# One level more of the fast product inside two of seven products, in ten slots of a gated FFN's last batch

## The chip, the cores and the metric

One core of one Trainium2 chip. The metric is the device time of one execution in microseconds (us). The kernel before took 711.19 us, the median of three runs (712.08, 711.18, 711.19). The profile is of one execution on the same core.

## The reference

A feed-forward layer with a gate, a conditioned norm ahead of it and 8-bit quantised hidden values behind it, cut to what matters:

```python
# x: (4, 1024, 512)   cond: (4, 128)   norm_w: (512, 128)
# up_w: (4096, 512)   down_w: (512, 2048)
scale = cond @ norm_w.T + 1.0
ms = jnp.mean(x * x, axis=-1, keepdims=True)
h = x * (scale[:, None, :] * jax.lax.rsqrt(ms + 1e-6))
u = h @ up_w.T
val, gate = jnp.split(u, 2, axis=-1)
h = val * jax.nn.gelu(gate, approximate=False)
# per token: 127 / max|h|, rounded and clipped, divided again
hq = act_quant(h)
# one scale for all: rounded to -1, 0, 1
wq = weight_quant(down_w)
return hq @ wq.T + x
```

## The kernel before, in words

The four batches (b = 0 to 3) of 1024 tokens go one after the other. A batch has 16 slots. A slot makes 128 of the 2048 hidden columns, gate and value, for all 1024 tokens: 2 x 2 blocks (gate or value, first or second 512 tokens) over an inner length of 512. Each slot uses one level of Winograd's form of Strassen's product: seven products of half the size in every direction instead of eight. A product is six matmuls of 128x128 weights with 512 tokens (`product`, L698 to L706; TERMS: each operand is split into a high and a low float16 part, of which three combinations count, times two halves of the inner length of 256). So a slot is 42 matmuls.

The steps of a slot are the methods of class `Slot` (L801 to L862). In the names below A, B and E are banks of PSUM, and v, t1 and t2 are float32 tiles of 128x512:

- `first` makes product 0 in A, and the scalar engine copies it to B (`first_copy`, L812). `fourth` makes product 4 in E, copied to v (L820). `fifth` adds product 5 onto A, copied to t2 (L827).
- `second` adds product 1 onto B: this is a gate half, whose Gelu goes to t1 (`second_gelu`, L834). `third` adds product 3 onto A. VectorE multiplies this value half by t1 and writes the hidden values H (`third_out`, L840).
- `gate` adds product 2 onto E, VectorE adds t2 (`gate_sum`, L848), and the scalar engine takes its Gelu (`gate_gelu`, L851). `value` adds product 6 onto A, VectorE adds v (`value_sum`, L857) and multiplies the two (`value_out`, L860).

`slot` (L864) writes these steps down in an order in which the first half of a slot stands between the second half of the one before. Each engine runs its instructions in the order of the code. Between the steps are places called x, y and z, into which other work is put. PSUM has two banks A, one B, two E and three that are called po, for the down projection.

While one batch runs, the batch before it is quantised and projected down. `pair_max` (L901) takes the largest absolute value over a pair of slots (L911), and merges it into a running maximum (L913). After the last pair GpSimd takes the maximum over the partitions (`token_max`, L927). VectorE makes the scales from it, and then multiplies each piece, two slots times 512 tokens, by them (`quant_scale`, L993). Either VectorE rounds the piece (`quant_round`, L997) or the scalar engine does in two steps (`quant_up`, L1001, `quant_down`, L1005). The down projection has small matmuls (L1070) over sums of such pieces (class `Pair`, L1049 to L1058). In the last batch only the sums are made beside the slots, for batch 2's projection, which runs in the tail behind the last slot. A class `Filler` (L1470) holds the maxima and pieces in a list with costs, and gives them out at x, y and z as its budget for a slot allows. GpSimd has nothing to do in the last batch's slots.

The parts of the weights wait in DRAM. `s_load_x` and `s_load_y` (L495 to L502) bring them in for each slot, some by a transposing DMA (L489), on the queue of SyncE (SP).

## Time and profile before

| | |
|---|---|
| runs | 712.08, 711.18, 711.19 us; median 711.19 |
| profiled execution | span 710.3 us from the first to the last instruction; the page gives no other time of it |
| median less span | 0.9 us |
| granted TensorE clock | 1.000 |
| busy: TensorE, VectorE, scalar engine, GpSimd | 703.8, 593.1, 421.9, 155.0 us |
| last batch's slots 0 and 4 begin at | 507.23, 543.50 us |
| a slot | 9.07 us |

The page's first part gives the busy time, the share of the span and the number of instructions of each engine (PE is TensorE, PEld its weight loads, DVE VectorE, ACT the scalar engine, POOL GpSimd). A group's row gives line, engine, operation, output and input tiles, shape, count, then busy us, mean ns of one, and the idle time ahead with what ended it. A timeline's row gives start, length, engine and line, and in brackets the idle time ahead of it and what released it. "issue" means that nothing which the profile shows was waited for.

### The profile page before, as it was taken

To read this page: it belongs to the slowest core of one execution; us is meant where nothing else is said; L and a number is where in the kernel's file an instruction comes from. 1 tells how busy PE (TensorE), PEld (TensorE's weight loads), DVE (VectorE), ACT (ScalarE), POOL (GpSimd) and SP (SyncE) were. 2 spreads that over 40 slices of the span, in tenths; PEclk is the share of its full clock that TensorE was granted. 3 is DMA by queue.
4 is the path that set the end of the run, shared out by engine and by line. 5 is a ranking of instruction groups with operands and counts; after the bars stand their busy time and mean duration, and the time that the engine had idled before them with its cause. 6 is when DMAs were issued, how large, how long until landed. Compare 5 with 4: busy or idle time off the path is not lost.

```text
span 710.3 us, 10162 instructions
## 1 busy us (share of the span) xinstructions
PE 703.8 (99%) x3620; PEld 355.3 (50%) x3620; DVE 593.1 (84%) x881; ACT 421.9 (59%) x714; POOL 155.0 (22%) x162
## 2 busy tenths in 40 slices
PE   8999999999999999999999999999999999999998
PEld 4544444444444446664444446665444444445854
DVE  7999878899888799998798868977688888755896
ACT  6987798975777754534336675544334665332473
POOL 1444535551200405430200033440020000000120
PEclk9999999999999999999999999999999999999999
DMA  7989999899776766479344555786744444442253
GB/s 261 324 270 252 254 188 263 217 207 227 264 135 163 179 178 172 136 174 225 118 118 105 133 126 150 191 188 141 207 105 105 104 105 97 99 101 90 105 178 119
DMA packets 223188, 120.26 MB, mean 169 GB/s; under 512 B 185353, under 2 KB 194589, under 8 KB 223138
## 3 DMA queue, kind: packets, MB, share of 16 engines
q1 hardware_dynamic: 222986, 119.49, 65.7%
q8 instruction: 28, 0.46, 0.3%
q14 instruction: 22, 0.18, 0.1%
q10 hardware_dynamic: 152, 0.13, 0.1%
HBM read 52.32 MB, written 23.09 MB: 106 GB/s over the span
## 4 chain that ended last, share of the span: by engine, by line
PE 97%; DVE 1%; ACT 1%; DMA 1%; issue 0%; ACTq 0%; SPq 0%
PE A L703 43%; PE E L703 21%; PE B L703 11%; PE po L1070 9%; PE po_end L1022 4%; PE pg L718 3%; PE pv L718 3%; PE pz L1194 1%; DMA s_dram<-s_rows 1%; PE ptx L1178 1%; PE pv L791 0%; PE po_B L1070 0%; PE pg L791 0%; PE pw L388 0%; PE po_E L1070 0%
## 5 line engine op out<-in xcount | busy, mean ns | idle before, releaser
L703 PEld LDWEIGHTS <-SXY 128*128 128x128 f16 x2268 | 221.9, 98 | 260.3
L703 PE MATMUL A<-R,SXY 128*128 128x512 f16 x1170 | 270.7, 379 | 0.0
L703 PE MATMUL E<-R,SXY 128*128 128x512 f16 x606 | 147.1, 379 | 0.0
L840 DVE SCALAR_TENSOR_TENSOR H<-A,sg,t 128x512 f32<-128x512 f32 x59 | 44.2, 749 | 61.2 <-PE A L703 56.9
L703 PE MATMUL B<-R,SXY 128*128 128x512 f16 x324 | 78.8, 379 | 0.0
L993 DVE TENSOR_TENSOR H<-H,am 128x1024 f32<-128x1024 f32 x64 | 76.5, 1217 | 0.0
L851 ACT ACTIVATE t<-t,sg 128x512 f32<-128x512 f32 x59 | 42.5, 719 | 57.0 <-DVE t L848 56.9
L911 DVE TENSOR_REDUCE gm<-H 128x512 f32<-128x1024 f32 x56 | 69.3, 1237 | 1.0
L927 POOL PARTITION_ALL_REDUCE am<-R x8 | 14.3, 1793 | 228.8 <-DVE R L913 228.8
L834 ACT ACTIVATE t<-B,sg 128x512 f32<-128x512 f32 x59 | 40.5, 686 | 36.9 <-PE B L703 36.9
L827 ACT COPY t<-A 128x512 f32<-128x512 f32 x59 | 34.3, 581 | 43.3 <-PE A L703 42.5
L820 ACT COPY v<-E 128x512 f32<-128x512 f32 x59 | 34.6, 586 | 33.5 <-PE E L703 30.0
L860 DVE SCALAR_TENSOR_TENSOR H<-v,sg,t 128x512 f32<-128x512 f32 x59 | 47.1, 800 | 7.3 <-ACT t L851 6.9
L812 ACT COPY B<-A 128x512 f32<-128x512 f32 x59 | 33.8, 573 | 32.4 <-PE A L703 32.0
L857 DVE TENSOR_TENSOR v<-A,v 128x512 f32<-128x512 f32 x59 | 40.4, 685 | 14.9 <-PE A L703 13.0
L1070 PE MATMUL po<-wd,R 128*128 128x256 fp8e4 x416 | 52.4, 273 | 0.0
L1070 PEld LDWEIGHTS <-R 128*128 128x128 bf16 (+1 forms) x448 | 43.8, 98 | 8.9
L848 DVE TENSOR_TENSOR t<-E,t 128x512 f32<-128x512 f32 x59 | 39.9, 678 | 6.6 <-PE E L703 6.6
L913 DVE TENSOR_TENSOR R<-R,gm 128x512 f32<-128x512 f32 x56 | 41.7, 745 | 1.1
L578 POOL TENSOR_SCALAR ssq<-ssq 128x2 f32<-128x2 f32 x12 | 5.4, 451 | 164.1 <-ACT xt L608 116.1
L1001 ACT ACTIVATE H<-H 128x1024 f32<-128x1024 f32 x33 | 34.7, 1051 | 5.2 <-DVE H L993 5.2
L1005 ACT ACTIVATE R<-H 128x1024 bf16<-128x1024 f32 x33 | 34.8, 1056 | 0.7
(249 smaller groups left out, 928.2 us busy)
## 6 DMA issues: line engine op xcount, KB each, us to landing
SXY<-s_dram SPq DMA_DIRECT2D x45, 256.0 KB, 3.0
SXY<-s_dram SPq DMA_DIRECT2D x51, 128.0 KB, 3.1
xr<-in_x_dram SPq DMA_DIRECT2D x19, 256.0 KB, 3.0
out_dram<-xr SPq DMA_DIRECT2D x19, 256.0 KB, 2.6
H<-in_L_cond_up_w_dram SPq DMA_DIRECT2D x9, 512.0 KB, 4.3
H<-in_x_dram SPq DMA_DIRECT2D x8, 512.0 KB, 6.2
s_dram<-s_rows SPq DMA_DIRECT2D x16, 256.0 KB, 2.7
s_dram<-SXY SPq DMA_DIRECT2D x4, 896.0 KB, 4.5
```

What stands on the lines that cost most here:

```text
L703: PE.matmul(o, s[:, w, k, :], operand(g // NJ, c, l, k), start=start and n == 0, stop=stop and n == len(TERMS) - 1, skip_group_check=True,)
L718: PE.matmul(ps, a[k // 2][:, w, k % 2, :], XP[:, l, k, h * TOK : (h + 1) * TOK], start=n == 0, stop=n == len(terms) - 1,)
L834: ACT.activation(self.t1, self.B, AF.Gelu, scale=gain(self.g, 1))
L840: DVE.scalar_tensor_tensor(h_half(self.g, 0), self.A, gain(self.g, 0), self.t1, ALU.mult, ALU.mult)
L848: DVE.tensor_tensor(self.t2, self.E, self.t2, ALU.add)
L851: ACT.activation(self.t2, self.t2, AF.Gelu, scale=gain(self.g, 1))
L857: DVE.tensor_tensor(self.v, self.A, self.v, ALU.add)
L860: DVE.scalar_tensor_tensor(h_half(self.g, 1), self.v, gain(self.g, 0), self.t2, ALU.mult, ALU.mult)
L911: DVE.tensor_reduce(gm[0], v, AX.X, ALU.max, apply_absolute_value=True)
L913: return [largest, lambda: DVE.tensor_tensor(m, m, gm[0], ALU.max)]
L993: DVE.tensor_tensor(v, v, r.to_broadcast([P, 2, TOK]), ALU.mult)
L1070: PE.matmul(po, w[:, j], m, start=start and j == 0, stop=stop and j == n - 1, skip_group_check=True,)
```

## The change

In slots 4 to 13 of the last batch, products 0 and 4 (of the seven) are no longer made by slot. Two neighbouring slots, an even and an odd one, are taken as a pair: their weights for such a product, side by side, are a matrix of 256 columns, the inner length is 256, and there are 512 tokens. That is again cut in two in each direction, and made by seven inner products (class `Inner`) of three matmuls each, 128x128 weights by 256 tokens. These 21 replace twice six of 512 tokens. Five pairs are made this way (`two_slots`).

The inner products need sums of the weights and the tokens, split into high and low parts once more. The tokens' sums are made once, for product 0 on VectorE (in batch 2's slot 15; the low part in slot 0) and for product 4 on GpSimd (sums behind slot 0, the low part behind slot 2); the scalar engine makes the high parts (`two_tokens`). The weights' sums are made for each pair, on GpSimd, one pair ahead (`two_weights`), from rows that `two_load` brings; in exchange `s_load_x` leaves out products 0 and 4 there. The inner sums take more copies on the scalar engine, and four additions of 128x256 a pair on VectorE (`lower_left`, `lower_right`).

In the last batch the pieces, maxima and sums no longer come from the `Filler` but from a list (`TWO_PLAN`), each with a slot and a place. Seven scalings of pieces go to GpSimd (`"scale"`). In a pair `gate` of the slot before comes ahead of its `third`, and `third` is cut in two. The banks A of the even slot, Z0 and Z4 are those of the down projection. Batch 2's maxima of slots 12 and 13 may start in slot 14's z, and not only in slot 15's x. Slot 14 takes its first two banks from the down projection's. The factor on the tokens X_UP is halved and the factor that undoes it doubled.

The diff, cut to its core:

```diff
--- before.py
+++ after.py
-X_UP = 2.0**8
+X_UP = 2.0**7
...
+    TWO = range(4, 14)
+    TWO_1 = TWO.start // 2
+
+    def in_two(g):
+        return g // NJ == B - 1 and g % NJ in TWO
 
     def s_load_x(g):
+        if in_two(g):
+            s_load(g, Y_TO + 1, C_ALL)
+            s_load(g, 1, Y_FROM, True)
+            return
...
-    def product(c, g, ps, start, stop):
+    def product(c, g, ps, start, stop, n0=0, n1=6):
...
-        for n, (w, l, k) in enumerate(TERMS):
+        for n, (w, l, k) in list(enumerate(TERMS))[n0:n1]:
...
         def first(self):
-            self.A = bank("A", 2, name=f"A_{self.g}")
+            if self.g == LAST * NJ + TWO.stop:
+                self.A, self.E = (po_bank(f"{n}_{self.g}") for n in "AE")
+            else:
+                self.A = bank("A", 2, name=f"A_{self.g}")
...
+    def two_load(c, m):
+        r, n = two_raw(c, m), PLACE[c]
+        for i in range(2):
+            j = block(LAST * NJ + 2 * m + i)
+            d = s_dram[j, :, n * 2 * HALF : (n + 1) * 2 * HALF]
+            if c == 0 or j in TURNED:
+                SP.dma_start(out=r[:, i].rearrange("p w f -> p (w f)"), in_=d)
+            else:
+                SP.dma_start_transpose(r[:, i].rearrange("p w (k f) -> p (w k) f", k=2), d)
+
+    def two_tokens(c, eng):
+
+        f, o = two["f"], two["T", c]
+        t = t_view(LAST)[:, :, c]
+        v = [t[:, :, n].rearrange("p a k t -> p k a t") for n in range(2)]
+        b11, b12, b21, b22 = (f[:, n] for n in range(4))
+
+        def whole():
+            w = f.rearrange("p (k h) t -> p k (h t)", k=2).rearrange("p k (a t) -> p k a t", t=P)
+            eng.tensor_tensor(w, v[0], v[1], ALU.add)
+
+        def sums():
+            eng.tensor_tensor(b22, b22, b12, ALU.subtract)
+            eng.tensor_tensor(b12, b12, b11, ALU.subtract)
+            eng.tensor_tensor(b11, b22, b11, ALU.add)
+            eng.tensor_tensor(b21, b21, b11, ALU.subtract)
+
+        def high():
+            ACT.copy(o[:, :, 0], f)
+
+        def low():
+            eng.tensor_tensor(o[:, :, 1], f, o[:, :, 0], ALU.subtract)
+
+        return whole, sums, high, low
+
+    def two_weights(c, m):
+
+        r, o = two_raw(c, m), two["W", c]
+        g = two["v"] if m == TWO_1 else two["g"]
+        g = g.rearrange("p (n f) -> p n f", n=4)
+        a11, a12, a21, a22 = (g[:, n] for n in range(4))
+        w = g.rearrange("p (j k) f -> p j (k f)", j=2)
+
+        def sums():
+            POOL.tensor_tensor(w, r[:, :, 0], r[:, :, 1], ALU.add)
+            POOL.tensor_tensor(a11, a11, a21, ALU.subtract)
+            POOL.tensor_tensor(a21, a21, a22, ALU.add)
+            POOL.tensor_tensor(a22, a22, a11, ALU.subtract)
+            POOL.tensor_tensor(a12, a12, a22, ALU.subtract)
+
+        def split():
+            ACT.copy(o[:, :, 0], g)
+            POOL.tensor_tensor(o[:, :, 1], g, o[:, :, 0], ALU.subtract)
+
+        return sums, split
...
+        def product(self, a, b, bank, half, start=False):
+            o = bank[:, half * HALF : (half + 1) * HALF].rearrange("p (a t) -> p a t", t=P)
+            for n, (w, l) in enumerate(((1, 0), (0, 1), (0, 0))):
+                PE.matmul(
+                    o, self.weight(a, w), self.tokens(b, l), start=start and n == 0, stop=n == 2,
+                    skip_group_check=True,
+                )
+
+        def first(self):
+            self.product("A11", "B11", self.Z, 1, True)
+            self.product("S3", "T3", self.Z, 0, True)
+
+        def first_copy(self):
+            m1 = self.Z[:, HALF:].rearrange("p (y o) -> p y o", y=1).to_broadcast([P, 2, HALF])
+            ACT.copy(self.out.rearrange("p (y o) -> p y o", y=2), m1)
+            ACT.copy(self.v, self.Z[:, :HALF])
+
+        def second(self):
+            self.product("A22", "T4", self.Z, 0)
+            self.product("S2", "T2", self.out, 1)
+            self.product("A12", "B21", self.out, 0)
+
+        def second_copy(self):
+            ACT.copy(self.u, self.out[:, HALF:])
+
+        def third(self):
+            self.product("S1", "T1", self.out, 1)
+
+        def lower_left(self, o):
+            DVE.tensor_tensor(o[:, :HALF], self.Z[:, :HALF], self.u, ALU.add)
+
+        def lower_right(self, o):
+            DVE.tensor_tensor(o[:, HALF:], self.out[:, HALF:], self.v, ALU.add)
+
+        def fourth(self):
+            self.product("S4", "B22", self.out, 1)
...
+        e.A = po_bank(f"A_{g}")
+        z4 = po_bank(f"Z4_{g}")
+        z0 = po_bank(f"Z0_{g}")
+        e.E = bank("E", 2, name=f"E_{g}")
+        o.A = bank("A", 2, name=f"A_{g + 1}")
+        o.v = wpool.tile([P, TOK], F32, name=f"v_{g + 1}", tag="v")
+        uv = wpool.tile([P, 2, HALF], F32, name=f"uv_{g}", tag="t1")
+        p0 = Inner(0, m, z0, e.A, uv)
+        p4 = Inner(4, m, z4, e.E, two["uv", 4])
+        p0.first()
+        p4.first()
+        p0.first_copy()
+        p4.first_copy()
+        prev.gate()
+        prev.gate_sum()
+        run("x")
+        p0.second()
+        p4.second()
+        w0[0]()
+        p0.second_copy()
+        p4.second_copy()
+        if more:
+            two_load(4, m + 1)
+        p0.third()
+        p0.lower_left(o.A)
+        p0.lower_right(o.A)
+        prev.third(0, 3)
+        p4.third()
+        p4.lower_left(o.v)
+        p4.lower_right(o.v)
+        prev.gate_gelu()
+        p0.fourth()
+        prev.third(3, 6)
+        e.first_copy()
+        w0[1]()
+        p4.fourth()
+        w4[0]()
+        prev.value_out()
+        prev.third_out()
+        run("y")
+        e.fifth()
+        e.fifth_copy()
+        e.v = two["v"]
+        ACT.copy(e.v, e.E)
+        e.second()
+        e.second_gelu()
+        run("z")
+        e.value()
+        e.value_sum()
+        o.first_copy()
+        if m + 2 < TWO.stop // 2:
+            two_load(0, m + 2)
+        even("loads")
+        e.gate()
+        e.gate_sum()
+        ran("x")
+        o.fifth()
+        o.fifth_copy()
+        o.E = bank("E", 2, name=f"E_{g + 1}")
+        ACT.copy(o.E, o.v)
+        e.gate_gelu()
+        e.value_out()
+        w4[1]()
+        o.second()
+        o.second_gelu()
+        ran("y")
+        e.third()
+        e.third_out()
+        o.value()
+        o.value_sum()
+        ran("z")
+        odd("loads")
...
+    TWO_PLAN = [
...
+        (6, "y", "piece", (4, 0), (5, 0)), (7, "x", "max", (2, 0)), (7, "z", "max", (2, 1)),
+        (5, "x", "scale", (2, 1)), (5, "z", "scale", (3, 1)),
...
+            after_pair = (14, "z") if (b, i) == (LAST - 1, 6) else (2 * i + 3, "x")
...
+        if b == LAST:
+            steps[0, "x"] = [(two_tokens(0, DVE)[3], (1.25, 0))]
+            steps[2, "x"] = [(two_tokens(4, POOL)[2], (0, 1.06))]
...
+                    two_tokens(0, POOL)[2]()
...
+            if b + 2 == B and j == NJ - 1:
+                two_places()
+                for c in (0, 4):
+                    two_load(c, TWO_1)
+                fs = two_tokens(0, DVE)
+                steps[NJ - 1, "x"] = [(fs[0], (1.25, 0)), (fs[1], (1.8, 0))]
...
+            if b + 1 == B and j == 0:
+                for f in two_tokens(4, POOL)[:2]:
+                    f()
+            if b + 1 == B and j == 1:
+                two_weights(0, TWO_1)[0]()
+            if b + 1 == B and j == 2:
+                two_tokens(4, POOL)[3]()
```

Rows of the kernel after carry the changed kernel's line numbers. The scalar engine around the last batch's slot 2 (slots are counted through the batches here, so this is 50; `two_t4` is the tile of the token sums for product 4, `two_n` the float32 sums ahead of the split). Before:

```order
L812 COPY B_50_4977<-A_50_4970 128x512
L820 COPY v_50_4986<-E_50_4979 128x512
L834 ACTIVATE t1_50_4994<-B_50_4977,sg_3_4828 128x512
L827 COPY t2_50_5011<-A_50_4970 128x512
L851 ACTIVATE t2_49_4943<-t2_49_4943,sg_3_4828 128x512
L812 COPY B_51_5044<-A_51_5037 128x512
L820 COPY v_51_5053<-E_51_5046 128x512
```

After:

```order
L826 COPY B_50_5004<-A_50_4997 128x512
L835 COPY v_50_5013<-E_50_5006 128x512
L849 ACTIVATE t1_50_5021<-B_50_5004,sg_3_4843 128x512
L934 CAST two_t4_4766<-two_n_4768 128x4x256
L842 COPY t2_50_5041<-A_50_4997 128x512
L866 ACTIVATE t2_49_4965<-t2_49_4965,sg_3_4843 128x512
L826 COPY B_51_5073<-A_51_5066 128x512
L957 CAST two_w0_4767<-two_n_4768 128x4x128
```

A cast of the token sums, which GpSimd makes, now stands ahead of the copy of A to t2 of slot 2, and the first of the weights' casts ahead of slot 3's copy of E.

GpSimd from the last rows of batch 3's tokens on (`am_2` is the maximum over the partitions, `ready` a dummy of the same operation, `two_r0` raw weight rows, `two_w0` the weights made from them; a row "ISA" without operands is an instruction that stands ahead of each change of kind). Before:

```order
L637 TENSOR_TENSOR H_79<-H_79 128x256 x4
L920 ISA
L920 ISA ready_108<-ready_108 128x1
L927 ISA am_2_4830<-R_78 128x512 x2
L920 ISA ready_108<-ready_108 128x1
L927 ISA am_3_5919<-R_78 128x512
L962 ISA am_3_5919<-row_0_6019 128x512
```

After:

```order
L1165 ISA am_2_4845<-R_78 128x512 x2
L925 ISA
L925 TENSOR_TENSOR two_n_4768<-R_78 128x1024
L928 TENSOR_TENSOR two_n_4768<-two_n_4768 128x256
L929 TENSOR_TENSOR two_n_4768<-two_n_4768 128x256
L930 TENSOR_TENSOR two_n_4768<-two_n_4768 128x256
L931 TENSOR_TENSOR two_n_4768<-two_n_4768 128x256
L950 TENSOR_TENSOR two_n_4768<-two_r0_4769 128x512
L951 TENSOR_TENSOR two_n_4768<-two_n_4768 128x128
L952 TENSOR_TENSOR two_n_4768<-two_n_4768 128x128
L953 TENSOR_TENSOR two_n_4768<-two_n_4768 128x128
L954 TENSOR_TENSOR two_n_4768<-two_n_4768 128x128
```

Where the queue went on to the dummy for the tail, there are now the sums of the tokens and the weights, behind an operand-less row of their own. The low part of the tokens (`two_t4`) follows the last of these rows.

VectorE in slots 6 and 7 (54 and 55 and on). Before:

```order
L848 TENSOR_TENSOR t2_53_5218<-E_53_5183,t2_53_5218 128x512
L857 TENSOR_TENSOR v_54_5261<-A_54_5245,v_54_5261 128x512
L860 SCALAR_TENSOR_TENSOR H_79<-v_53_5190,sg_3_4828,t2_53_5218 128x512
L993 TENSOR_TENSOR H_79<-H_79,am_2_4830 128x2x512
L997 TENSOR_SCALAR R_78<-H_79 128x4x256
L840 SCALAR_TENSOR_TENSOR H_79<-A_54_5245,sg_3_4828,t1_54_5269 128x512
L906 TENSOR_REDUCE R_78<-H_79 128x512 x2
L911 TENSOR_REDUCE gm_3_1_0_5349<-H_79 128x512
L848 TENSOR_TENSOR t2_54_5289<-E_54_5254,t2_54_5289 128x512
L857 TENSOR_TENSOR v_55_5330<-A_55_5314,v_55_5330 128x512
L860 SCALAR_TENSOR_TENSOR H_79<-v_54_5261,sg_3_4828,t2_54_5289 128x512
```

After, behind slot 7's maxima, up to the even slot of the next pair (`Z0`, `Z4`: banks of inner products, `uv`: copies of inner products):

```order
L863 TENSOR_TENSOR t2_55_5475<-E_55_5477,t2_55_5475 128x512
L1011 TENSOR_TENSOR A_57_5520<-Z0_56_5518,uv_56_5522 128x256
L1014 TENSOR_TENSOR A_57_5520<-A_56_5516,uv_56_5522 128x256
L1011 TENSOR_TENSOR v_57_5521<-Z4_56_5517,two_n_4768 128x256
L1014 TENSOR_TENSOR v_57_5521<-E_56_5519,two_n_4768 128x256
L875 SCALAR_TENSOR_TENSOR H_79<-v_55_5334,sg_3_4843,t2_55_5475 128x512
L855 SCALAR_TENSOR_TENSOR H_79<-A_55_5333,sg_3_4843,t1_55_5489 128x512
L1231 TENSOR_TENSOR H_79<-H_79,am_2_4845 128x2x512
L1235 TENSOR_SCALAR R_78<-H_79 128x4x256
L1231 TENSOR_TENSOR H_79<-H_79,am_2_4845 128x2x512
L1235 TENSOR_SCALAR R_78<-H_79 128x4x256
L872 TENSOR_TENSOR two_n_4768<-A_56_5516,two_n_4768 128x512
```

The pieces stood one at a time between the outputs of slots. Now two stand together, scaled and rounded, behind the outputs of the odd slot, and four additions of 128x256 stand ahead of those.

146 lines of the change are left out of this document (125 added, 21 removed), and 13 rows, old and new, of the table TWO_PLAN.

## The prediction

> **What bounds the kernel now.** I read the page first, then the chain that ended last, then busy time by stretch in the last batch, then the groups by form, and last the timelines of the places that the change touches. The page:
>
> ```profile
> span 710.3 us, 10162 instructions
> PE 703.8 (99%) x3620; PEld 355.3 (50%) x3620; DVE 593.1 (84%) x881; ACT 421.9 (59%) x714; POOL 155.0 (22%) x162
> PE 97%; DVE 1%; ACT 1%; DMA 1%; issue 0%; ACTq 0%; SPq 0%
> ```
>
> TensorE is busy 99% of the span and 97% of the chain. So every stall that the change makes on PE is added in full, and every matmul that it saves is saved in full. The chain's pieces give the price of a matmul of each width (start, length, engine, line, count):
>
> ```profile
> 533.29 2.59 PE A L703 x12
> 652.43 1.75 PE po L1070 x16
> ```
>
> A 128x512 product matmul takes 2.59 / 12 = 0.216 us. The 256-column matmuls of the down projection take 1.75 / 16 = 0.109. Two slots of the last batch, one of those that the change rewrites first and one of the last (bounds, length, then busy time of PE, PEld, DVE, ACT, POOL):
>
> ```profile
> 545.12:554.19 9.07, 9.07 (x44) 4.12 (x42) 8.34 (x9) 5.81 (x9) 0.00 (x0) 1.00 0.44 104
> 617.68:626.75 9.07, 9.07 (x43) 4.09 (x42) 6.58 (x10) 3.16 (x6) 0.00 (x0) 1.00 0.45 101
> ```
>
> PE has no gap in either. VectorE stands at 8.34 of 9.07 in the first: it is the next engine to be late. GpSimd is idle throughout, at a granted clock of 1.00.
>
> **What it removes.** A pair of slots had 84 matmuls of 512 columns. It gets 60, and 42 of 256. That is 84 x 0.216 = 18.13 us before and 60 x 0.216 + 42 x 0.109 = 17.54 after (unrounded quotients): 0.59 a pair, 2.95 for five pairs. The profiled execution's span is 710.3, and the median of the runs, 711.19, lies 0.9 above it. Without any stall the time would be 711.19 - 2.95 = 708.24. A narrow matmul would have to take 0.1234 for the gain to be nothing (42 x 0.0141 = 0.59). Against that: each matmul of the row at 652.43 has a weight load of its own too, as the inner ones have, and 0.109 held.
>
> **What it adds on VectorE, in a pair.** The rows (count, busy, mean ns of one, idle before):
>
> ```profile
> L840 DVE SCALAR_TENSOR_TENSOR H<-A,sg,t 128x512 f32<-128x512 f32 x59 | 44.2, 749 | 61.2 <-PE A L703 56.9 <-ACT s_rows L459 2.0 <-DMA wd<-in_L_cond_down_w_dram 1.5
> L848 DVE TENSOR_TENSOR t<-E,t 128x512 f32<-128x512 f32 x59 | 39.9, 678 | 6.6 <-PE E L703 6.6
> L857 DVE TENSOR_TENSOR v<-A,v 128x512 f32<-128x512 f32 x59 | 40.4, 685 | 14.9 <-PE A L703 13.0 <-ACT H L328 1.3 <-issue 0.5
> L860 DVE SCALAR_TENSOR_TENSOR H<-v,sg,t 128x512 f32<-128x512 f32 x59 | 47.1, 800 | 7.3 <-ACT t L851 6.9
> L911 DVE TENSOR_REDUCE gm<-H 128x512 f32<-128x1024 f32 x56 | 69.3, 1237 | 1.0
> L913 DVE TENSOR_TENSOR R<-R,gm 128x512 f32<-128x512 f32 x56 | 41.7, 745 | 1.1
> L993 DVE TENSOR_TENSOR H<-H,am 128x1024 f32<-128x1024 f32 x64 | 76.5, 1217 | 0.0
> L997 DVE TENSOR_SCALAR R<-H 128x1024 bf16<-128x1024 f32 x31 | 22.4, 721 | 1.0
> L442 DVE TENSOR_TENSOR H<-H 128x256 f32<-128x256 f32 x25 | 11.1, 445 | 1.5 <-issue 0.9
> ```
>
> The fullest pairs (slots 4 to 9) have two of each slot step (2 x 2.91 = 5.82), four inner sums of 128x256 (at 0.445: 1.78), two pieces scaled and rounded (3.88) and two maxima (3.96): 15.4 us of 17.54. That fits only because seven scalings go to GpSimd. The order puts both pieces, 3.9 us, in one run behind the outputs of the slot before: from 8.4 to 12.3 us into the pair. value_sum, due at 11.1, then ends at 13.0, and the first product that waits for it (the even slot's third) starts at 14.9. Scalar engine: at most 2 x 5.81 of the first window, six more copies of at most 0.57 (row 508.78 below) and two casts of that size, 16.2 of 17.54: no bound. Pairs 5 and 6 have less of everything.
>
> **What it adds on GpSimd.**
>
> ```profile
> L627 POOL TENSOR_TENSOR xn<-xn,sc 128x512 f32<-128x512 f32 x8 | 10.0, 1270 | 10.2 <-ACT xn L626 10.2
> L727 POOL TENSOR_TENSOR H<-R 128x1024 f32<-128x1024 f16 x2 | 4.4, 2214 | 0.0
> L637 POOL TENSOR_TENSOR xt<-xn,xt 128x256 f32<-128x256 f32 x5 | 4.0, 794 | 0.4
> ```
>
> For the next pair it makes two weights (1.27 whole, four quarter sums of 128x128 at about half of 0.794, 1.27 for the low part: 4.1 to 4.3 each) and two scalings at about 2.21: 12.7 to 13.1 us. Laid end to end with the casts and loads that it waits for, the low part of product 4's weights ends 17.7 us after the pair's start, and PE takes it at 17.54 + 0.98 = 18.5: 0.8 to spare. The raw rows for it come by two transposing loads:
>
> ```profile
> 534.61 1.40 SPq L489 DMA_TRANSPOSE SXY<-s_dram  x1
> 536.69 1.19 SPq L489 DMA_TRANSPOSE SXY<-s_dram  x1
> SXY<-s_dram SPq DMA_DIRECT2D x51, 128.0 KB, 3.1
> ```
>
> Issued from 4.6 us on at 1.2 to 1.4 each, and landing some 3 us later, they are there at about 9, where GpSimd reaches for them at 8.9. What else SP carries there is less than before. Cost 0; 0.3 if late, inside the 0.8.
>
> **Entry, first place: token sums on VectorE in batch 2's slot 15.** There it gets one 128x1024 (VectorE's own L993 takes 1.22; 1.3 for this one) and four 128x256 (1.78) between the slot's maxima and gate_sum. The maxima of slots 12 and 13 move ahead into an idle stretch.
>
> ```profile
> 504.21 1.22 DVE L911 TENSOR_REDUCE gm<-H 128x512 f32<-128x1024 f32 x1
> 507.37 0.67 DVE L848 TENSOR_TENSOR t<-E,t 128x512 f32<-128x512 f32 x1
> 508.78 0.57 ACT L812 COPY B<-A 128x512 f32<-128x512 f32 x1
> 516.56 0.69 DVE L857 TENSOR_TENSOR v<-A,v 128x512 f32<-128x512 f32 x1 [0.60 <-PE A L703]
> ```
>
> From 504.21: 3.1 + 0.7 (the L913 left behind) = 508.0 where gate_sum stood at 507.37. Its Gelu and the copy behind it on the scalar engine follow, so the copy ends at 510.05 and not 509.35, where the second product wants it at 509.82: stall 0.2 (0 to 0.7). The low part, 1.2 more in slot 0, eats the idle 0.60 at 516.56 and leaves the batch's last maximum 0.6 late.
>
> **Entry, second place: GpSimd's way back from the all-reduce.** Token sums for product 4 stand right behind the all-reduce of the maxima, and the first instruction there is one with no operands, which the program also has at each earlier change between the two kinds of GpSimd work.
>
> ```profile
> 167.06 0.38 POOL L920 PARTITION_ALL_REDUCE ready<-ready  x1 [5.81 <-issue]
> 237.85 1.21 POOL L578 TENSOR_SCALAR ssq<-ssq 128x2 f32<-128x2 f32 x1 [48.83 <-ACT xt L608]
> 482.08 0.38 POOL L920 PARTITION_ALL_REDUCE ready<-ready  x1 [6.57 <-issue]
> 520.01 1.78 POOL L927 PARTITION_ALL_REDUCE am<-R  x1 [2.73 <-DVE R L913]
> 532.03 0.59 ACT L827 COPY t<-A 128x512 f32<-128x512 f32 x1 [1.84 <-PE A L703]
> ```
>
> Going to the all-reduce, GpSimd stood 5.81 and 6.57 us with nothing to wait for. Going back, the change lies under 48.83 us of other idling and can't be read. Bounds 0 to 6.57; I take 6.2, from the same kind of change in the other direction. [...] With 6.2: the all-reduce ends at 520.01 + 1.78 + 0.6 = 522.4, the sums begin at 528.6, take 2.21 + 4 x 0.79 and end at 534.0. The scalar engine's cast of them stands ahead of slot 2's copy t<-A, at 532.03 in the row. The cast takes 1.05 (twice 0.57, less the start), so that copy ends at 535.6. The value product, which writes over the bank that is copied, starts the 2.59 at 533.29, 533.5 with the first stall. Stall 2.1 (0 to 2.5). Without the 6.2 the cast is done before the copy is due, and nothing is lost.
>
> **Both engines at once.** GpSimd now works through slots 4 to 12 beside VectorE. The rows where they met before:
>
> ```profile
> 270.18 3.52 POOL L627 TENSOR_TENSOR H<-H,sc 128x512 f32<-128x512 f32 x2 [0.84 <-ACT H L626]
> 270.29 2.29 DVE L674 TENSOR_TENSOR H<-xt,H 128x1024 f16<-128x1024 f32 x1
> 485.79 1.22 DVE L674 TENSOR_TENSOR nx<-xt,nx 128x1024 f16<-128x1024 f32 x1
> 442.52 3.29 POOL L637 TENSOR_TENSOR H<-H 128x256 f32<-128x256 f32 x4
> 444.49 0.74 DVE L860 SCALAR_TENSOR_TENSOR H<-v,sg,t 128x512 f32<-128x512 f32 x1
> 445.14 1.22 DVE L913 TENSOR_TENSOR R<-R,gm 128x512 f32<-128x512 f32 x1
> ```
>
> The L674 beside a running GpSimd row took 2.29 where one alone took 1.22, and the L913 took 1.22 for its 0.745; the L860 a moment before lost nothing. So a meeting costs VectorE 0 to 1.1 us. A heavy pair has six such two-operand instructions (two each of L860, L913, L993). Taken in turn, GpSimd's last row ends at 19.35 instead of 17.7, 0.9 after PE wants it, in three pairs; and at the entry a value_out behind a scaling of 2.21 makes gate_sum late by up to 1.85. Bounds 0 to 2.7 + 1.85 = 4.55. I take 0.7: about half of the 0.9 in one pair and a little at the entry. One of the three meetings shows no loss, and most of a loss falls into VectorE's 2.1 and GpSimd's 0.8 of slack.
>
> **Last pairs and tail.** The three old sums of batch 2 move to slots 12 to 14, four instructions each:
>
> ```profile
> L1049 DVE TENSOR_TENSOR sq<-R 128x1024 bf16<-128x1024 bf16 x2 | 1.4, 685 | 0.0
> ```
>
> VectorE has there 5.82 + 1.78 + 3.96 + 2 x 4 x 0.69 = 17.1 of 17.54 in the last pair, the fullest. Slot 14's first banks are taken from the down projection's, which are free. Cost 0, for the tail's products of batch 2 lie ahead of the last output; if they didn't, one output of 0.75.
>
> Sum: 708.24 + 0.2 + 2.1 + 0.7 = 711.24, so 711.3.
>
> **The rivals.**
>
> 1. *No change to tell* (forecast, 0.38): 711.3. Its own range is 709.8 to 712.6.
> 2. *Faster* (0.33): the way back costs GpSimd little or is done ahead while it waits, and the meetings are absorbed: 708.24 + 0.2 + 0 to 0.7 and up to 0.5 of a short change back, 708.4 to 709.7, most likely 709.0. [...] Against: both visible changes cost about 6.
> 3. *Slower* (0.29): one resource serves GpSimd and VectorE's two-operand instructions in turn. Price 0.9 in each of three pairs and 1.85 at the entry. Without the stall of the way back 708.24 + 0.2 + 4.55 = 713.0, with it 715.1; middle 714. It decides from the point where a meeting costs GpSimd more than the 0.8 it has spare in a pair. For it: 2.29 against 1.22. Against: 0.74 at 444.49. [...]
>
> That the change doesn't do what it says (0.1234 for a narrow matmul) lies inside 1 and 3: 2.95 more, with a chance too small to be named apart.
>
> **How the numbers follow.** The predicted time is the first case's, 711.3. From no change one can tell about 0.2%, 1.42 us: the bounds are 709.77 and 712.61. The ends of case 2 and case 3 give 708.4 to 715.1; leaving out the lowest tenth and highest tenth, 708.6 to 714.2. Faster 0.33, same 0.38, slower 0.29.
>
> **What would show it.** PE's rows: inner products of 0.109 a matmul, five pairs of 17.54. GpSimd's idle time ahead of the first token sum: 6 is my case, under 4 the second. A gap of about 2 in PE in slot 2 ahead of the value product, with the copy of A as releaser, and none of over 0.3 in slots 6 to 15. Waits of PE on GpSimd's low weights at the start of the pairs at slots 6, 8 and 10, with VectorE's L913 or L860 at 1.2 or more, would be the third case. Wrong altogether would be narrow matmuls over 0.12, or VectorE late in every pair.

## The result and the profile after

| | before | after |
|---|---|---|
| median of the runs, us | 711.63 (711.18 to 712.32, 4 runs) | 722.28 (720.89 to 722.73, 4 runs) |
| ratio to before | | 1.0141, 95% interval 1.0126 to 1.0156 |
| span of the profiled execution, us | 710.3 | 720.2 |
| granted TensorE clock, mean | 1.000 | 0.995 |

The changed kernel is 1.4% slower. The range given was 708.6 to 714.2: the prediction was wrong by 11 us. Each ratio further down is to runs of the kernel before that were taken beside that run (their medians are 711.98 to 712.38). In the runs of both kernels that list their span the time lies about 1.8 us above it (after: 721.99 and 720.2), so the spans' difference, 9.9 us, is the difference of two times. It is taken apart here. The page of the kernel after:

```profile
span 720.2 us, 10533 instructions
PE 704.9 (98%) x3710; PEld 364.5 (51%) x3710; DVE 613.4 (85%) x904; ACT 431.9 (60%) x748; POOL 234.1 (33%) x235
PE 86%; DVE 6%; POOL 4%; issue 2%; ACT 1%; DMA 1%; SPq 0%; POOLq 0%; DVEq 0%; ACTq 0%
```

The chain that ended last was 97% TensorE; now VectorE, GpSimd and time that nothing shown accounts for stand in it with 12% together. Busy time by stretch of the kernel after (bounds, length, busy PE, PEld, DVE, ACT, POOL, clock): slots 2 and 3 around the first stall, then the five pairs, each from its first inner product to the next one's:

```profile
533.50:542.60 9.10, 4.83 (x12) 1.62 (x11) 4.64 (x7) 2.15 (x3) 7.69 (x9) 0.66 0.04 10
550.93:569.62 18.69, 17.86 (x103) 9.88 (x102) 17.09 (x20) 11.92 (x22) 16.01 (x14) 1.00 0.45 99
569.62:588.03 18.41, 17.71 (x103) 9.91 (x102) 17.68 (x20) 12.31 (x21) 16.50 (x16) 1.00 0.48 101
588.03:607.50 19.47, 18.03 (x104) 9.89 (x103) 19.19 (x24) 12.24 (x22) 17.07 (x15) 1.00 0.45 95
607.50:625.97 18.47, 17.86 (x104) 9.97 (x103) 16.37 (x20) 11.49 (x21) 12.87 (x14) 1.00 0.39 86
625.97:643.51 17.54, 17.54 (x104) 9.98 (x103) 14.31 (x22) 8.21 (x16) 0.38 (x1) 1.00 0.45 99
```

The last pair has the forecast 17.54 exactly. There GpSimd has nothing left to do, and VectorE has its old sums and maxima. The four pairs beside which GpSimd works are 1.15, 0.87, 1.93 and 0.93 longer: 4.88 together. The other loss stands ahead of them. The timeline of TensorE there (start, length, line, and the idle time ahead with its releaser):

```profile
537.96 5.28 PE L712 MATMUL A<-R,SXY 128*128 128x512 f16 x12 [4.27 <-ACT t L842]
```

TensorE stood 4.27 us in slot 2, waiting for the copy of A, and then took 5.07 us to the start of its next product (543.03) for twelve matmuls that take 2.59 elsewhere, and 0.13 more for the next six: the granted clock of that stretch is 0.66. The stall cost 0.16 more than it shows: the product starts at 537.96, and right behind the six matmuls before it (532.23, 1.30) it would have started at 533.53, 4.43 earlier. So the entry costs 4.43 + 2.48 + 0.13 = 7.04. GpSimd and the scalar engine in the same place:

```profile
521.00 1.78 POOL L1165 PARTITION_ALL_REDUCE am<-R  x1 [2.33 <-DVE R L1151]
529.83 2.11 POOL L925 TENSOR_TENSOR two_n<-R 128x1024 f32<-128x1024 f16 x1 [7.05 <-ACT v L835]
533.63 1.58 POOL L930 TENSOR_TENSOR two_n<-two_n 128x256 f32<-128x256 f32 x1
536.38 1.04 ACT L934 CAST two_t<-two_n 128x1024 f16<-128x1024 f32 x1 [5.79 <-POOL two_n L931]
537.33 0.58 ACT L842 COPY t<-A 128x512 f32<-128x512 f32 x1
```

GpSimd starts the sums 7.05 us behind the all-reduce, two of the quarter sums take 1.58 and 1.06 instead of 0.72 (VectorE scales and rounds a piece beside them), and the scalar engine's cast stands ahead of the copy for 5.79 us. The trace names the copy L835 as what released the sums. That needed an experiment, since no such need stands in the code.

The sum: 7.04 + 4.88 - 2.95 = 8.97, or 9.0 of the 9.9. Of the rest 0.4 was there at 200 us already, far ahead of the slots that were changed, and 0.5 lies behind the last output's addition. The two kernels' last VectorE rows are 9.36 apart, which is the 0.4 and the 8.97: nothing else was lost on the way, in slots 14 and 15 or in the tail.

What in the pairs is late? VectorE's groups by form between 543.5 and 634 us of the kernel before, which are the same ten slots, and then between 551 and 644 us of the kernel after (count, busy, mean ns):

```profile
L993 DVE TENSOR_TENSOR H<-H,am 128x1024 f32<-128x1024 f32 x13 | 15.5, 1218 | 0.0
L860 DVE SCALAR_TENSOR_TENSOR H<-v,sg,t 128x512 f32<-128x512 f32 x10 | 7.5, 750 | 1.9 <-ACT t L851 1.9
L913 DVE TENSOR_TENSOR R<-R,gm 128x512 f32<-128x512 f32 x9 | 6.2, 689 | 0.2
L997 DVE TENSOR_SCALAR R<-H 128x1024 bf16<-128x1024 f32 x4 | 2.8, 694 | 0.1
```

```profile
L1235 DVE TENSOR_SCALAR R<-H 128x1024 bf16<-128x1024 f32 x8 | 10.9, 1373 | 0.2
L1151 DVE TENSOR_TENSOR R<-R,gm 128x512 f32<-128x512 f32 x9 | 10.8, 1201 | 0.3
L1231 DVE TENSOR_TENSOR H<-H,am 128x1024 f32<-128x1024 f32 x6 | 8.6, 1428 | 0.0
L875 DVE SCALAR_TENSOR_TENSOR H<-two_n,sg,t 128x512 f32<-128x512 f32 x5 | 7.5, 1496 | 1.0 <-ACT t L866 1.0
L863 DVE TENSOR_TENSOR t<-E,t 128x512 f32<-128x512 f32 x10 | 6.8, 684 | 1.2 <-PE E L712 1.1
L1149 DVE TENSOR_REDUCE gm<-H 128x512 f32<-128x1024 f32 x9 | 11.1, 1233 | 0.0
```

Four kinds got longer: the merge of maxima (L1151, 1.20 where it was 0.69 in these slots), the output of the even slots (L875, 1.50, was 0.75), the scaling (L1231, 1.43, was 1.22) and the rounding (L1235, 1.37, was 0.69). The first three read two operands from SBUF; the fourth reads one and writes SBUF. L863, with one operand in PSUM, and the reduction L1149 stayed as they were (0.684 and 1.233 where they had been 0.683 and 1.236). What TensorE then waited for, between 480 and 722 us:

```profile
PE A L712 <- ACT t L842: 4.9, 2, 4.3
PE Z L985 <- POOL two_n L958: 1.3, 3, 0.7
PE A L985 <- DVE A L1014: 1.0, 2, 0.7
PE Z L985 <- ACT uv L997: 0.7, 2, 0.4
```

TensorE waited for GpSimd's low weights (1.3 us), for VectorE's inner sums (1.0), and for the scalar engine's inner copies behind late VectorE rows (0.7). The first row is the entry's 4.27 and a wait of 0.66 in the first pair, which is of the entry's kind: a cast of the weights (L957) stood ahead of the copy of A and waited for GpSimd's sums, which ended at 560.67. Each of these waits costs about 0.16 more than it shows: the first pair has waits of 0.17 and 0.66, and 0.17 + 0.66 + 2 x 0.16 is its 1.15; the second has one of 0.70, and 0.70 + 0.16 is 0.86 of its 0.87.

### The profile page after: what moved, and what is told of

Read it like the earlier page. It is cut to its first block, busy times and chain, and to the rows that moved or that the text cites. A ratio compares the mean times of both kernels' runs of the same rounds, so it can differ in the third digit from the quotient of the medians.

```text
span 720.2 us, 10533 instructions
## 1 busy us (share of the span) xinstructions
PE 704.9 (98%) x3710; PEld 364.5 (51%) x3710; DVE 613.4 (85%) x904; ACT 431.9 (60%) x748; POOL 234.1 (33%) x235
## 4 chain that ended last, share of the span: by engine, by line
PE 86%; DVE 6%; POOL 4%; issue 2%; ACT 1%; DMA 1%; SPq 0%; POOLq 0%; DVEq 0%; ACTq 0%
PE A L712 36%; PE E L712 18%; PE po L1308 9%; PE B L712 9%; PE po_end L1260 4%; PE pg L727 3%; PE pv L727 3%; DVE R L1151 1%; DVE gm L1149 1%; DVE H L1231 1%; PE pz L1432 1%; DMA s_dram<-s_rows 1%; DVE H L875 1%; PE Z L985 1%; PE ptx L1416 1%
## 5 line engine op out<-in xcount | busy, mean ns | idle before, releaser
L712 PEld LDWEIGHTS <-SXY 128*128 128x128 f16 x2148 | 210.9, 98 | 249.6 <-issue 9.6
L712 PE MATMUL A<-R,SXY 128*128 128x512 f16 x1110 | 261.9, 382 | 4.9 <-ACT t L842 4.9
L712 PE MATMUL E<-R,SXY 128*128 128x512 f16 x546 | 132.7, 379 | 0.0
L1149 DVE TENSOR_REDUCE gm<-H 128x512 f32<-128x1024 f32 x56 | 69.2, 1236 | 0.7
L1231 DVE TENSOR_TENSOR H<-H,am 128x1024 f32<-128x1024 f32 x57 | 69.7, 1241 | 0.0
L826 ACT COPY B<-A 128x512 f32<-128x512 f32 x59 | 33.8, 573 | 39.7 <-PE A L712 36.0
L872 DVE TENSOR_TENSOR v<-A,v 128x512 f32<-128x512 f32 x54 | 37.0, 686 | 18.6 <-PE A L712 16.7
L1151 DVE TENSOR_TENSOR R<-R,gm 128x512 f32<-128x512 f32 x56 | 46.9, 838 | 1.3
L875 DVE SCALAR_TENSOR_TENSOR H<-v,sg,t 128x512 f32<-128x512 f32 x54 | 42.9, 796 | 5.2 <-ACT t L866 4.8
L835 ACT COPY v<-E 128x512 f32<-128x512 f32 x49 | 28.7, 585 | 25.7 <-PE E L712 23.5
L863 DVE TENSOR_TENSOR t<-E,t 128x512 f32<-128x512 f32 x59 | 40.0, 679 | 3.1 <-PE E L712 2.8
L712 PEld LDWEIGHTS <-R 128*128 128x128 f16 x210 | 20.5, 98 | 25.7 <-issue 1.0
L1239 ACT ACTIVATE H<-H 128x1024 f32<-128x1024 f32 x29 | 30.5, 1052 | 4.4 <-DVE H L1231 4.2
```

Of the source, the lines that this page charges most:

```text
L712: PE.matmul(o, s[:, w, k, :], operand(g // NJ, c, l, k), start=start and n == 0, stop=stop and n == len(TERMS) - 1, skip_group_check=True,)
L863: DVE.tensor_tensor(self.t2, self.E, self.t2, ALU.add)
L872: DVE.tensor_tensor(self.v, self.A, self.v, ALU.add)
L875: DVE.scalar_tensor_tensor(h_half(self.g, 1), self.v, gain(self.g, 0), self.t2, ALU.mult, ALU.mult)
L1149: DVE.tensor_reduce(gm[0], v, AX.X, ALU.max, apply_absolute_value=True)
L1151: return [largest, lambda: DVE.tensor_tensor(m, m, gm[0], ALU.max)]
```

## The experiments

The theory after the result: the entry loses 7.0 (6.9 in the expectations below) by an in-order wait (cast behind GpSimd's way back and sums) and TensorE's clock behind it; the pairs lose 4.9 because GpSimd's reads and some VectorE instructions hold each other up. Rivals: the way back is no cost of its own but a wait for L835; GpSimd merely has too much to do; VectorE merely has too much to do.

**The way back alone (p1).** In the kernel before:

```diff
         POOL.partition_all_reduce(am[:, c], m_view(b, h), P, bass_isa.ReduceOp.max)
+        if b == 2 and h == 1:
+            POOL.tensor_tensor(probe[:, :1], probe[:, :1], probe[:, 1:], ALU.add)
```

> The kernel before with one added GpSimd addition of 128x1, on a tile of its own that nothing else uses, behind the all-reduce of batch 2's maxima; it has nothing to wait for. Theory (the way back from the all-reduce costs GpSimd its time whatever is waited for): it starts 6 to 7.1 us behind the end of the all-reduce, as the token sums did. Rival (the token sums waited for a semaphore, the trace names the scalar engine's copy L835): it starts within 1 us. Time in both 711.6, for nothing waits for it.

GpSimd's timeline of that kernel:

```profile
519.41 1.78 POOL L929 PARTITION_ALL_REDUCE am<-R  x1 [2.73 <-DVE R L913]
528.18 0.20 POOL L931 TENSOR_TENSOR probe<-probe 128x1 f32<-128x1 f32 x1 [6.99 <-issue]
534.69 0.38 POOL L922 PARTITION_ALL_REDUCE ready<-ready  x1 [6.31 <-issue]
```

An addition that needs nothing started 6.99 us behind the all-reduce, and the next all-reduce 6.31 us behind it. So the way back took about as much as the way there, and it accounts for the 7.05 without L835, whose copy ended at 529.13, 0.70 ahead of the sums. In x2 below the same sums start 7.62 us behind the all-reduce, and there the trace names no releaser. The time was 711.48, one run.

**The entry without the wait (e1).** In the changed kernel:

```diff
-            if b + 1 == B and j == 0:
-                for f in two_tokens(4, POOL)[:2]:
-                    f()
```

> The changed kernel without GpSimd's sums of the tokens for product 4: the cast in slot 2 takes the sums for product 0, which lie there (batch 3's output is not the reference's). The cast, its place, the low part and all else stay. Theory (the cast waits for GpSimd's way back and its sums, and TensorE's half clock comes from that stall): no stall in slot 2, granted clock 1.00 there, 6.9 us less; GpSimd's weights then come about 6.5 us sooner too, at 545.7 instead of 552.2, where a pair without a stall would want the low ones at 544.5: 0 to 1.5 lost there. 715.4 to 716.9. Rival (the stall has to do with the cast or its copy themselves, or the clock falls there for another reason): 720 or more.

717.21 us, ratio 1.0073 (1.0058 to 1.0087): 5.1 less than the changed kernel, and 0.3 above the range that was expected. The stretch that had the clock of 0.66, in this kernel:

```profile
533.50:542.60 9.10, 7.80 (x37) 3.47 (x36) 8.84 (x10) 2.92 (x5) 4.75 (x3) 1.00 0.42 101
```

The 4.27 stall is gone, and with it the low clock. In its place came 1.30 ahead of slot 3's product on E (VectorE's L863; VectorE is busy 8.84 of the 9.10 us above, and GpSimd's low part of the token sums runs from 533.00 to 535.12) and 1.55 at the first pair (GpSimd's low weights, done at 548.0, wanted at 546.5). So the token sums were not the whole of the entry: the weights behind the same way back are late too, by less, and the wait for L863 was not expected.

**Two slots later (s1).** The same work with `TWO = range(6, 14)`, cast, low part and first weights two slots later.

> The split starts with slot 6 instead of slot 4 (four pairs), and the cast of the token sums, their low part and the first weights stand two slots later; all results are the reference's. Theory (the entry loses 6.9 us, 4.3 by the cast that waits for GpSimd in front of the copy of A and 2.6 by TensorE's half clock behind that stall; the pairs lose 4.9 to GpSimd and VectorE meeting): the entry's 6.9 are gone, the first pair's 1.15 too, and 0.59 of gain is given up: 722.3 - 6.9 - 1.15 + 0.59 = 714.8, still over before's 711.6, with a granted clock of 1.00 in slots 0 to 5. Rival (it is VectorE's sums in slot 15 and slot 0 or the loads that make slot 2 late): the stall in slot 2 stays, and the time is about 721.

718.1 us, ratio 1.0081 (1.0066 to 1.0096). The stall in slot 2 and the low clock are gone, as expected (mean clock 1.000). But the time is 3.3 over what was expected, and TensorE's waits say why:

```profile
PE Z L985 <- POOL two_n L958: 2.5, 2, 1.8
PE E L712 <- DVE t L863: 1.8, 1, 1.8
```

The plan's two pieces for slot 4 now stood in a slot outside the pairs (a plain slot from here on), ahead of its gate_sum: 1.8. And the first pair's low weights were late by 1.8, since they had been put two slots later together with the pair.

**GpSimd's share in the pairs (x1, x2, x3).** Three kernels leave out GpSimd's scalings, its weight sums from the second pair on, or both:

```diff
-        "scale": lambda i, h, am: quant_scale(LAST - 1, i, h, am, POOL),
+        "scale": lambda i, h, am: None,
...
-        w0 = two_weights(0, m + 1) if more else (nothing,) * 2
-        w4 = two_weights(4, m + 1) if more else (nothing,) * 2
+        w0 = (nothing,) * 2
+        w4 = (nothing,) * 2
```

> The changed kernel without the seven scalings on GpSimd (those pieces are rounded unscaled, so batch 2's output is not the reference's). Pairs at slots 4, 6, 8, 10, 12 took 18.69, 18.41, 19.47, 18.47 and 17.54 us. Theory (VectorE and GpSimd hold each other up where VectorE reads two operands): the weight sums still meet VectorE, so L1151 and L875 stay stretched in places, but GpSimd is no longer late: excess over 17.54 falls from 4.9 to 1.5 or less in all, 718.9 or less. Rival A (GpSimd only has too much to do): excess 0, and VectorE's rows at their old lengths or not makes no difference. Rival B (VectorE has too much to do by itself): nothing changes, 722.3.

> The changed kernel in which GpSimd makes the weights' sums for the first pair alone, and the later pairs use them again (batch 3's output is not the reference's). GpSimd has only two scalings a pair then. Theory (meetings): L1151 and L875 fall back to 0.69 and 0.75 nearly everywhere, excess 1 or less in all, 718.4 or less. Rival A (GpSimd too long): excess 0. Rival B (VectorE too long by itself): 722.3.

> The changed kernel with neither the scalings on GpSimd nor the weights' sums beyond the first pair (outputs of batches 2 and 3 are not the reference's). GpSimd is idle from slot 4 on, VectorE's own work is as in the changed kernel. Theory: all pairs take 17.54, VectorE's rows have the lengths of before (L1151 0.69, L875 0.75, L1231 1.22, L1235 0.72), 722.3 - 4.9 = 717.4, the rest being the entry. Rival B (VectorE too long by itself): most of the 4.9 stays.

| | time, us | ratio (interval) | first four pairs, us |
|---|---|---|---|
| after | 722.28 | 1.0141 (1.0126 to 1.0156) | 18.69, 18.41, 19.47, 18.47 |
| x1, no scalings | 717.80 | 1.0078 (1.0063 to 1.0093) | 18.70, 17.53, 17.54, 17.53 |
| x2, no sums | 726.61 | 1.0203 (1.0188 to 1.0218) | 26.42, 17.54, 17.53, 17.54 |
| x3, neither | 716.42 | 1.0065 (1.0048 to 1.0082) | 17.53, 17.54, 17.54, 17.53 |

With GpSimd idle all pairs have 17.54 and VectorE's rows their old lengths (between 551 and 625 us of x3):

```profile
L1231 DVE TENSOR_TENSOR H<-H,am 128x1024 f32<-128x1024 f32 x6 | 7.3, 1217 | 0.0
L1151 DVE TENSOR_TENSOR R<-R,gm 128x512 f32<-128x512 f32 x8 | 5.5, 693 | 0.3
L1235 DVE TENSOR_SCALAR R<-H 128x1024 bf16<-128x1024 f32 x8 | 5.4, 691 | 0.2
```

So VectorE's own work fits, which ends that rival. x3 is 5.9 faster than the changed kernel, 4.9 of it in the pairs and most of the rest in a shorter stall of slot 2 (3.65).

x1 stayed within its expectation, but doesn't tell the theory from the rival that GpSimd has too much to do. Two of VectorE's groups between 551 and 625 us of x1:

```profile
L1231 DVE TENSOR_TENSOR H<-H,am 128x1024 f32<-128x1024 f32 x6 | 10.4, 1731 | 0.0
L1235 DVE TENSOR_SCALAR R<-H 128x1024 bf16<-128x1024 f32 x8 | 9.4, 1179 | 0.2
```

These rows were stretched beside the weights' sums, and still only the first pair is longer, by its waits of 0.17 and 0.66 as in the changed kernel. The later pairs absorb the sums alone, and their 3.7 us come only with the scalings. Against that rival stands GpSimd's own time. At the least lengths that its rows have in the changed kernel (a weight 1.15 + 4 x 0.45 + 1.16, a scaling 2.35) two weights and two scalings are 12.9 us of 17.54, as forecast. In the second and third pairs the same rows add up to 16.4 and 16.6 us: 3.5 and 3.7 of stretch, where the forecast had 0.8 to spare.

The x2 result went against its expectation by 8 us, and shows the meetings best. Without the weights between them, the seven scalings ran in one go, and VectorE's two whole pieces fell among them (GpSimd, then VectorE, in x2):

```profile
552.02 19.51 POOL L1231 TENSOR_TENSOR H<-H,am 128x1024 f32<-128x1024 f32 x7
```

```profile
560.58 2.71 DVE L1231 TENSOR_TENSOR H<-H,am 128x1024 f32<-128x1024 f32 x1
563.33 2.73 DVE L1235 TENSOR_SCALAR R<-H 128x1024 bf16<-128x1024 f32 x1
565.98 3.36 DVE L1231 TENSOR_TENSOR H<-H,am 128x1024 f32<-128x1024 f32 x1
569.37 2.71 DVE L1235 TENSOR_SCALAR R<-H 128x1024 bf16<-128x1024 f32 x1
572.01 0.68 DVE L872 TENSOR_TENSOR two_n<-A,two_n 128x512 f32<-128x512 f32 x1
```

Four VectorE rows of 3.8 us together took 11.5, each about the length of one GpSimd scaling, and GpSimd's took 2.79 each on average, where the shortest in the changed kernel has 2.35. That the two went in turn, a whole instruction at a time, is an estimate from these lengths; no row shows it. TensorE waited 6.49 us, not for anything that GpSimd makes but for VectorE's L872 behind these rows, and the twelve matmuls behind that wait took 4.39 instead of 2.59 (granted clock 0.87 in that pair). Over the four pairs GpSimd had about a third of its work in the changed kernel, though more of it in this one pair (19.5 us), and the pair was 7.7 us longer. So what decides here is what GpSimd's work falls beside, and not its amount over the pairs.

**Meetings alone, in the kernel before (c1, c2).** GpSimd gets work that nobody uses, in slots 4 to 9 behind the slot's first output; five multiplications (c1) or eight memsets (c2):

```diff
+                t = state["idle"]
+                POOL.tensor_tensor(probe[:, :1], h_half(g - 1, 0)[:, :1], h_half(g - 1, 0)[:, 1:2], ALU.add)
+                for _ in range(5):
+                    POOL.tensor_tensor(t, t, t, ALU.mult)
```

> The kernel before with five GpSimd multiplications of a 128x512 float32 tile of their own in each of the last batch's slots 4 to 9, behind that slot's first output; nothing else uses them. Theory (meetings of GpSimd's reads with VectorE's two-operand instructions): L860, L913 and L993 stretch beside them by 0.4 to 1.2 each and L840, L848, L857 and L911 do not; VectorE, at 8.3 to 8.7 of 9.07 in these slots, is late, and the slots take 0.3 to 1.2 longer each: 713.4 to 719. Rival (no meetings, GpSimd only had too much to do): 711.6 and no row longer.

> The same with eight GpSimd memsets of that tile for each five multiplications: GpSimd writes and doesn't read. [...] If any work on GpSimd holds VectorE up: as with the multiplications.

c1 took 715.84 us, ratio 1.0055 (1.0040 to 1.0070); c2 712.15, ratio 1.0002 (0.9992 to 1.0011), where the theory had 711.6 to 712.5. VectorE's groups between 545 and 605 us of c1, then between 545 and 600 us of c2:

```profile
L995 DVE TENSOR_TENSOR H<-H,am 128x1024 f32<-128x1024 f32 x12 | 18.5, 1568 | 0.0
L860 DVE SCALAR_TENSOR_TENSOR H<-v,sg,t 128x512 f32<-128x512 f32 x7 | 7.9, 1124 | 1.7 <-ACT t L851 1.7
L913 DVE TENSOR_TENSOR R<-R,gm 128x512 f32<-128x512 f32 x6 | 5.8, 967 | 0.1
L999 DVE TENSOR_SCALAR R<-H 128x1024 bf16<-128x1024 f32 x4 | 5.1, 1269 | 0.1
L840 DVE SCALAR_TENSOR_TENSOR H<-A,sg,t 128x512 f32<-128x512 f32 x6 | 4.5, 747 | 1.6 <-PE A L703 1.6
```

```profile
L995 DVE TENSOR_TENSOR H<-H,am 128x1024 f32<-128x1024 f32 x12 | 14.3, 1216 | 0.0
L860 DVE SCALAR_TENSOR_TENSOR H<-v,sg,t 128x512 f32<-128x512 f32 x7 | 5.3, 752 | 1.7 <-ACT t L851 1.7
L913 DVE TENSOR_TENSOR R<-R,gm 128x512 f32<-128x512 f32 x6 | 4.1, 688 | 0.1
L999 DVE TENSOR_SCALAR R<-H 128x1024 bf16<-128x1024 f32 x4 | 3.5, 864 | 0.1
```

Beside GpSimd work that reads, the same four kinds grow as in the changed kernel, the rounding too, which the expectation had not named; L840, with an operand in PSUM, does not grow (0.747, before 0.751). Nothing waits for GpSimd here, and c2 has the same small addition ahead of its memsets, so this loss belongs to the meetings alone. It is 3.9 us; four waits of TensorE for gate_sum (0.51 to 0.96, 3.1 together, and 0.16 more for each) make 3.8 of it. That ends the rival that GpSimd merely has too much to do as the whole cause. Beside writes only the rounding grows, 0.69 to 0.86, and the time stays; GpSimd was busy with the memsets for 26 us, with the multiplications for 40. So the two-operand rows grew beside the work that reads (L995 1.568 in c1) and not beside the work that only writes (1.216 in c2). Why the rounding grows beside both, to 1.269 and 0.864, was not shown.

**The scalings back on VectorE (d1).**

```diff
-        "scale": lambda i, h, am: quant_scale(LAST - 1, i, h, am, POOL),
+        "scale": lambda i, h, am: quant_scale(LAST - 1, i, h, am),
```

> The changed kernel with its seven scalings back on VectorE, at the places where GpSimd had them; one part of the change undone, the results are the reference's. Theory (meetings): GpSimd does only the weights' sums, the waits of TensorE on its low weights go, but VectorE's own work is 15.4 + 2 x 1.22 = 17.9 of 17.54 in each of the three fullest pairs, plus 0.5 to 1 of meetings with the sums: excess 0.9 to 1.4 each, 2.7 to 4.2 in all, where it was 4.9; with the entry's 6.9 unchanged 720.1 to 721.6. Rival (the scalings on GpSimd are worth their place, meetings cost little): VectorE alone is late by more than the 4.9, 722.3 or more.

725.39 us, ratio 1.0188 (1.0175 to 1.0201): slower still, and within the rival's bounds, though not because meetings cost little. The pairs took 18.95, 20.24, 20.67 and 20.30, 10.0 together over 17.54 each, where 2.7 to 4.2 had been expected. Of the third:

```profile
588.35:609.02 20.67, 17.86 (x103) 9.96 (x102) 20.39 (x25) 12.25 (x22) 12.24 (x13) 1.00 0.47 88
```

VectorE is busy 20.39 of 20.67: it is the bound there. Its own work was put at 17.9 in such a pair; the weights' sums, which remain on GpSimd, stretch it on top (L1231 takes 1.70 on average). So the scalings cost less on GpSimd than they would on VectorE, and either place is too full.

**Laid out anew (v1, v2, v3).** No scalings on GpSimd, fewer pairs, pieces spread over plain slots and over the scalar engine, the cast in slot 3, for four pairs (v1, v3 with a smoother plan) or three (v2).

```diff
-    TWO = range(4, 14)
+    TWO = range(6, 14)
...
+        (4, "x", "scale", (2, 0), (2, 1)), (4, "z", "scale", (3, 0)), (4, "z", "max", (1, 0)),
+        (5, "x", "scale", (3, 1), (4, 0)), (5, "z", "scale", (4, 1)), (5, "z", "max", (1, 1)),
```

> Four pairs from slot 6 on, no scalings on GpSimd, one piece rounded on the scalar engine for each on VectorE, the cast of the token sums in slot 3, first weights in slot 4; all results are the reference's. Theory: no wait behind the way back, so no stall in slots 2 and 3 and the full clock; GpSimd has only the weights' sums in the pairs (8.4 of 17.5), so no wait on low weights; VectorE has 14.7 and at most 1.5 of meetings in a pair: excess 0 to 0.4 each. 711.6 - 4 x 0.59 + 0.3 to 1.5 = 709.5 to 710.7. Rival (the entry costs whatever is moved, or the split itself costs in its copies and banks): 712 or more.

> The same from slot 8 on: three pairs, two more plain slots for the pieces. Theory: 711.6 - 3 x 0.59 + 0 to 0.7 = 709.8 to 710.5. Rival: 711.6 or more.

> Four pairs from slot 6 on as in the planned kernel from slot 6, with its plan smoothed: less in slots 3 to 5 (1.16 and 1.53 us of stalls there), three scalings and one or two rounds in a pair instead; all results are the reference's. Theory: VectorE 15.9 of 17.54 in the first three pairs and up to 1.5 of meetings: 0 to 0.4 late each; slots 2 to 5 lose 0.3 to 1. 711.9 - 2.36 + 0.3 to 2.2 = 709.8 to 711.7. Rival (the work that the split adds has no room on VectorE however it is laid): 712.5 or more.

713.91 (ratio 1.0029, 1.0018 to 1.0040), 714.48 (1.0047, 1.0032 to 1.0062) and 714.79 us (1.0041, 1.0028 to 1.0054): all three better than the changed kernel by about 8 us, none better than before, and none where the theory put it. In v1 the first three pairs took 18.06, 17.53 and 17.54. The loss had gone into the plain slots ahead of them:

```profile
PE E L712 <- DVE t L863: 1.7, 3, 1.2
PE B L712 <- ACT B L826: 1.5, 1, 1.5
PE A L985 <- DVE A L1014: 0.4, 1, 0.4
```

There GpSimd made its token sums and first weights beside VectorE's scalings (one of 1.22 took 3.12), and the scalar engine had the rounds and casts; one cast of weights waited 2.20 for GpSimd's sums, with the copy of A to B (L826) behind it. With 0.16 for each wait these are about 4.4, against a gain of 4 x 0.59 = 2.36: + 2.0, and 1.9 was measured. v3 moved the stall to slot 5 (2.03 in its profile, with a granted clock of 0.91 from 543 to 562 us; the profile is of the slowest of its runs). A plan that wins was not found.

## Why the prediction was wrong, point by point

The profiles differ by 9.9 us where next to nothing was forecast. The second entry made 4.9 of it beyond its term (7.0 for 2.1), the meetings 4.2 (4.9 for 0.7), and 0.9 lies outside the change; the first entry's 0.2 did not come. The other 1.2 of the 11 us is not in the profiles: the medians differ by 10.7, and the kernel before has 711.63 where 711.19 was taken.

1. *TensorE bounds, 0.59 a pair: right.* 17.54 was measured in the last pair of the changed kernel and in every pair of x3, and 0.109 for a narrow matmul held.
2. *First entry, 0.2 of 0 to 0.7: within its bounds, its mechanism not seen.* The changed kernel's profile shows no stall there. v1 shows 0.24 and v3 0.26, but TensorE waits there for gate_sum itself and not for the copy behind its Gelu.
3. *Second entry, 2.1 of 0 to 2.5: the right wait, but three times the cost; this term failed first.* The way back was 7.05 where 6.2 was taken and 6.57 was the most (p1: 6.99 with nothing to wait for). The sums took 6.5 where 5.4 was taken, beside VectorE's rows. All began 0.4 later. That makes 4.4 us of stall. And the slow clock behind it, 2.6, stood nowhere in the sum. e1 shows that both hang on the wait: without it no stall stood there and the clock was 1.00. The stall was longer with a longer way back: with 7.05 (after) and 7.62 us (x2) of it the stall shown is 4.27 and 5.07.
4. *Both engines at once, 0.7 of 0 to 4.55: the step that failed.* It was weighed by one unstretched L860 against two stretched rows, and the slack of 2.1 and 0.8 was to absorb most. 4.88 was lost in the pairs alone, more than the upper bound had for them (2.7). Three things were missing or too small. The rounding, which reads a single operand, meets GpSimd too (0.69 became 1.37). GpSimd's own rows were stretched by 3.5 and 3.7 us in the second and third pairs, where the working had 1.65 at the most (19.35 for 17.7). And waits ended on the scalar engine and on inner sums, for which the working had no term. The 1.85 that the upper bound had for gate_sum at the entry is hidden in the changed kernel by the longer stall; without the stall it appears, as the 1.30 in e1. The third rival, at 0.29, rested on such meetings, and even its upper value, 715.1, is 7.2 short: 2.6 of that is the clock, 2.3 the longer stall, the rest the pairs and what lies outside the change.
5. *Loads, last pairs, tail, banks: as forecast*, nothing was lost there up to the last output.

Of what should have shown it, "a gap of about 2 in PE in slot 2" came at the named place with the named releaser, but as 4.27, and in place of "none of over 0.3 in slots 6 to 15" there were five, of 0.32 to 0.70. The signs of the third case came: waits for GpSimd's low weights at slots 6 (0.70) and 8 (0.39), though none at 10, and the merges and outputs at 1.20 and 1.50.

## What to carry to other kernels

In a kernel whose main engine is busy 99%, price work that is moved to an idle engine by what it falls beside. In x2 the VectorE rows beside GpSimd's scalings took 2.71 to 3.36 us instead of 0.69 and 1.22, about the 2.79 that one scaling took there: price about such a length for each pair of instructions that can fall together, and the growth of the other engine's rows too (2.79 for GpSimd's, where 2.35 is the shortest in the changed kernel). In an in-order queue put no instruction that waits for another engine ahead of a copy that the main engine needs soon: here TensorE waited 4.27 for it in slot 2, 0.66 in the first pair and 1.53 in v1. And to a stall of TensorE of some 4 us add the slow matmuls behind it (here twelve in 5.07 instead of 2.59). A saving of 0.59 us in 18 on the bounding engine is worth having only if the next engine's 85% doesn't have to pay for it.
